# Row scatters kept out of values' products, empty rows scattered between the first expert blocks, silu in place

## The chip, the cores and the metric

The kernel runs on one core of a Trainium2 chip. Its time is the device time of one execution in microseconds; the time of a kernel is the median over its runs. PE is TensorE, DVE is VectorE, ACT is ScalarE, POOL is GpSimd and SP is SyncE. A name such as L705 is a line of the kernel before, which is also the line that its profile shows; the changed kernel's lines lie a few numbers off.

## The reference

The input x has 16 batches of 512 tokens of 256 numbers. The reference normalizes each token and adds to x an attention layer and a mixture of experts, both fed by the normalized tokens:

```python
xn = _layernorm(x, axis=-1)
x = x + _L0_attn_ref(xn, ...) + _L0_ffn_ref(xn, ...)

# attention: 16 heads of 16, rotary q and k, causal softmax
scores = einsum('bqhd,bkhd->bhqk', q, k) * scale          # masked above the diagonal
out = einsum('bhqk,bkhd->bqhd', softmax(scores), v).reshape(B, S, H * Dh)
return out @ Wo.T

# experts: 32 experts of hidden size 128, the best 4 of each token, and a shared expert of 512
topk_scores, topk_idx = top_k(softmax(flat @ router_w.T + router_bias), 4)
h = silu(einsum('nd,ehd->neh', flat, gate_w)) * einsum('nd,ehd->neh', flat, up_w)
out = (sel * topk_scores[:, :, None]).sum(axis=1)         # sel: the 4 chosen experts' outputs
out = out + silu(flat @ sgate_w.T) * (flat @ sup_w.T) @ sdown_w.T
```

Everything is float32.

## The kernel before

**One order for all.** The order of the work on every engine is written out by hand. The program is a sequence of some 350 rounds, and `for r in range(last)` emits them one after the other. A round begins with `cut()` and `scores(r)`: products of queries and keys for the attention (L840, twice: `sq` to find the row maxima on DVE, `sk` transposed to be exponentiated by ACT into a tile `pe`). `cut()` has GpSimd zero what lies above the diagonal in the `pe` of the round before (L866). Then come steps that were put into a round by `at(r, cost, step)`, and between them steps of the list `fill`, taken as they fit a level of PE work per round. Each engine has its own queue and works through it in order; SyncE's queue issues most of the DMAs, in order too.

**Attention.** A batch takes 20 rounds for `scores`, in two halves of heads `p`. Twelve rounds later `values(b, p, c)` multiplies the `pe` tiles by the values `va` (L886, 32 matmuls), for one quarter `c` of the heads at a time. These products fall into two of every ten rounds.

**Routing and scattering.** In rounds 0 to 35 tokens are normalized and routed, and each token's row of 265 numbers (the token, its four experts, their weights, its number) goes to `xn_d` in HBM. The experts' rows lie one expert after the other in `xs`, in half blocks of 128 rows. From round `R_SCATTER` = 36 to round 127 rows are scattered into `xs`: `reload(b)` has SyncE bring a batch's rows back into one of three `rows` tiles (L551), and puts 16 scatters of 128 rows each on the list `waiting`; `scatter(n)` has GpSimd issue the next n of these (L560, indirect DMAs). The counts per round are spread evenly:

```python
rows_in_all, rounds = B * NT * TOPK + E, R_MOE - 2 - R_SCATTER
at(R_MOE - 2 - rounds // 6, 0.0, scatter_empty)
n = (r + 1) * rows_in_all // rounds - gone
```

The `E` = 32 scatters at the end are `scatter_empty`: for each expert, an empty row is written to the unused rows of its last half block (`gaps`), so that these rows belong to a token number that doesn't count. PE works on attention and on the shared expert (`gate_up` L246, `down` L258, whose tokens come as `sxt` through SyncE, L233) in these rounds.

**Blocks.** At round `R_MOE` = 130 `begin_blocks` starts 144 blocks of 256 rows, two half blocks with an expert each. For block n, SyncE reads the rows `xb` from `xs` (`fetch_rows`, L640, five tiles) and the two experts' weights `w` (`fetch`, L647, four tiles); PE transposes (L654), multiplies by gate and up (L667), and by down (L691); GpSimd adds the results to `moe` in HBM with accumulating indirect DMAs (`add_up`, L705). The step `first(n)` issues, in this order, the rows of block n+4, the weights of block n+2, the sums of block n-3, and gate and up of block n. Blocks follow on each other until round 302, where the sums are combined and the last batches of attention are done.

**silu.** `glu` (L277 to L282) is used by the shared expert and by the blocks: ACT makes the tanh `th` (L279), DVE makes `gs` out of it (L281) and the product out of `gs` (L282).

Of the kernel before, what the change touches and what calls it, by code (L numbers as in the profile page):

```python
# [11 lines left out]
F32 = mybir.dt.float32  # L12
# [5 lines left out]
ALU = mybir.AluOpType  # L18
# [4 lines left out]
P = 128  # L23
B, S, D = 16, 512, 256
NT = S // P
T = B * NT
NH, DH, HP = 16, 16, 32
# [4 lines left out]
BLK, BC = 2 * HB, 2  # L32
# [40 lines left out]
def block_kernel(ctx: ExitStack, tc, x, wqkv, wo, rope, rw, rb, wexp, sg, su, sd, out):  # L73
# [202 lines left out]
    def glu(dst, ps, name):  # L276

        th = spool.tile([P, 2 * P], F32, tag="th", name=f"th_{name}", bufs=2)
        nc.scalar.activation(th, ps[:, 0, :], AF.Tanh, scale=0.5)  # L279
        gs = spool.tile([P, 2 * P], F32, tag="gs", name=f"gs_{name}", bufs=2)  # L280
        nc.vector.scalar_tensor_tensor(gs, th, 1.0, ps[:, 0, :], ALU.add, ALU.mult)  # L281
        nc.vector.scalar_tensor_tensor(dst, gs, 0.5, ps[:, 1, :], ALU.mult, ALU.mult)  # L282

    def interleaved_shared(halves, late=False, sums=None, xt=None):

# [190 lines left out]

    empty = epool.tile([P, ROW], F32, tag="empty", name="empty", bufs=1)
    nc.vector.memset(empty, 0.0)  # L480
    nc.gpsimd.tensor_copy(empty[:, ID_AT : ID_AT + 1].bitcast(I32), ids[:, T : T + 1])
    none = epool.tile([P, D], F32, tag="none", name="none", bufs=1)
# [74 lines left out]
    def scatter(most):  # L557
        for _ in range(min(most, len(waiting))):
            n, index, row = waiting.pop(0)
            nc.gpsimd.indirect_dma_start(  # L560
                out=views[n % NVIEWS],
                out_offset=bass.IndirectOffsetOnAxis(ap=index, axis=0),
                in_=row,
                in_offset=None,
            )

    def scatter_empty():
        waiting.extend((e, gaps[:, e : e + 1], empty) for e in range(E))


    def block_tables():
# [62 lines left out]
    def expert_steps(pool):  # L634

        w, xb, xt, ht, wrow, ybs, who = {}, {}, {}, {}, {}, {}, {}

        def fetch_rows(n):
            xb[n] = pool.tile([P, BC, ROW], F32, tag="xb", name=f"xb_{n}", bufs=5)
            nc.sync.dma_start(  # L640
                xb[n], xs[n * BLK : (n + 1) * BLK, :].rearrange("(c p) d -> p c d", p=P)
            )

        def fetch(n):
            w[n] = pool.tile([P, BC, 3 * D + 1], F32, tag="w", name=f"w_{n}", bufs=4)
            for c, e in enumerate(on_sync(where[n % P : n % P + 1, n // P, :], E - 1)):
                nc.sync.dma_start(w[n][:, c, :], wexp[bass.ds(e * P, P), :])  # L647

        def turned(n):
            pt = bank([P, 2, BLK], f"pxt_{n}")  # L650
            rows = xb[n]
            for c in range(BC):
                for dc in range(2):
                    nc.tensor.transpose(  # L654
                        pt[:, dc, c * P : (c + 1) * P], rows[:, c, dc * P : (dc + 1) * P], ident
                    )
            xt[n] = pool.tile([P, 2, BLK], F32, tag="xbt", name=f"xbt_{n}", bufs=2)
            nc.scalar.copy(xt[n], pt)  # L658

        def gate_up(n):  # L660
            pg = bank([P, 2, BLK], f"pg_{n}")
            rows = xt.pop(n)
            for u in range(2):
                for c in range(BC):
                    for dc in range(2):
                        at = (2 * u + dc) * H
                        nc.tensor.matmul(  # L667
                            pg[:, u, c * HB : (c + 1) * HB], lhsT=w[n][:, c, at : at + H],
                            rhs=rows[:, dc, c * HB : (c + 1) * HB],
                            start=(dc == 0), stop=(dc == 1),  # L670
                        )
            ht[n] = pool.tile([P, BLK], F32, tag="ht", name=f"ht_{n}", bufs=2)
            glu(ht[n], pg, f"e{n}")

            four = pool.tile([P, BC, TOPK], F32, tag="four", name=f"four_{n}", bufs=2)
            for c in range(BC):
                nc.vector.scalar_tensor_tensor(  # L677
                    four[:, c, :], xb[n][:, c, E_AT : E_AT + TOPK], w[n][:, c, 3 * D :],
                    xb[n][:, c, W_AT : W_AT + TOPK], ALU.is_equal, ALU.mult,
                )  # L680
            wrow[n] = pool.tile([P, BC], F32, tag="wrow", name=f"wrow_{n}", bufs=3)
            nc.vector.tensor_reduce(wrow[n], four, AX.X, ALU.add)

            who[n] = pool.tile([P, BC], I32, tag="who", name=f"who_{n}", bufs=6)
            nc.vector.tensor_copy(who[n], xb.pop(n)[:, :, ID_AT].bitcast(I32))

        def down(n):
            py = bank([P, BC, D], f"py_{n}")
            h = ht.pop(n)
            for c in range(BC):  # L690
                nc.tensor.matmul(  # L691
                    py[:, c, :], lhsT=h[:, c * P : (c + 1) * P], rhs=w[n][:, c, 2 * D : 3 * D],
                    start=True, stop=True,
                )
            w.pop(n)
            yb = pool.tile([P, BC, D], F32, tag="yb", name=f"yb_{n}", bufs=4)
            weight = wrow.pop(n)
            for c in range(BC):
                nc.scalar.mul(yb[:, c, :], py[:, c, :], weight[:, c : c + 1])  # L699
            ybs[n] = yb  # L700

        def add_up(n):
            yb, at = ybs.pop(n), who.pop(n)
            for c in range(BC):
                nc.gpsimd.indirect_dma_start(  # L705
                    out=moe[c],
                    out_offset=bass.IndirectOffsetOnAxis(ap=at[:, c : c + 1], axis=0),
                    in_=yb[:, c, :], in_offset=None, compute_op=ALU.add,
                )

        def first(n):
            if n == -2:
                for k in range(4):
                    fetch_rows(k)
                for k in range(2):
                    fetch(k)
            if 0 <= n + 4 < NBLK and n >= 0:
                fetch_rows(n + 4)
            if 0 <= n + 2 < NBLK and n >= 0:
                fetch(n + 2)  # L720
            if 0 <= n - 3 < NBLK:
                add_up(n - 3)
            if 0 <= n < NBLK:
                gate_up(n)

        out = []
        for n in range(-2, NBLK + 3):
            out.append((1.75 if 0 <= n < NBLK else 0.0, lambda n=n: first(n)))
            if 0 <= n + 2 < NBLK:
                out.append((0.45, lambda n=n: turned(n + 2)))  # L730
            if 0 <= n - 1 < NBLK:
                out.append((0.9, lambda n=n: down(n - 1)))
        return out
# [147 lines left out]
    def values(b, p, c):  # L881
        po = bank([P, S], f"po_{b}_{p}_{c}")
        for k in range(NT):
            j, col = PLACE_K[c, k]
            for g in range(4):
                nc.tensor.matmul(  # L886
                    po[g * HP : (g + 1) * HP, k * P :],
                    lhsT=va[b % 2][k][:, 8 * p + 4 * c + g, :],
                    rhs=pes[b, p, j, g // 2][:, g % 2, col : col + S - k * P],
                    start=(k == 0), stop=(k == NT - 1), skip_group_check=True,  # L890
                )
        oc = work.tile([P, S], F32, tag="oc", name=f"oc_{b}_{p}_{c}")
        nc.scalar.copy(oc, po)
        pos_o[b, p, c] = oc
# [51 lines left out]
            stores.append((half(out_v, b, i2), xr))  # L946


    events = {}

    def at(r, cost, step):
        events.setdefault(r, []).append((cost, step))
# [24 lines left out]
    for b in range(B):  # L977
        for p in range(2):
            r = 20 * b + 10 * p
            at(r + 10, 0.45, lambda b=b, p=p: maxima(b, p))  # L980
            for c, rv in ((0, r + LAG + 7), (1, r + LAG + 11)):
                at(rv, 2.3, lambda b=b, p=p, c=c: values(b, p, c))
                at(rv + 1, 0.45, lambda b=b, p=p, c=c: normalized(b, p, c))
            at(r + LAG + 13, 0.45, lambda b=b, p=p: turned(b, p))
        for i2 in range(2):
# [29 lines left out]
    empty_rows, experts = block_tables()  # L1015
    at(R_SCATTER + 5, 0.0, empty_rows)
    at(R_SCATTER + 7, 0.0, experts)
    rows_in_all, rounds = B * NT * TOPK + E, R_MOE - 2 - R_SCATTER
    for b in range(B):

        last = R_SCATTER + b * NT * TOPK * rounds // rows_in_all - 1
# [2 lines left out]
        at(first, 0.0, lambda b=b: place(b))  # L1024
        at(second, 0.0, lambda b=b: placed(b))
        at(R_SCATTER + max(0, b - 2) * NT * TOPK * rounds // rows_in_all, 0.0, lambda b=b: reload(b))
    at(R_MOE - 2 - rounds // 6, 0.0, scatter_empty)
    gone = 0
    for r in range(rounds):
        n = (r + 1) * rows_in_all // rounds - gone  # L1030
        at(R_SCATTER + r, 0.0, lambda n=n: scatter(n))
        gone += n

# [3 lines left out]
    at(R_LAST - 4, 0.0, load_late)  # L1037

    def begin_blocks():
        scatter(len(waiting))  # L1040
        stages.pop("rows").close()
        stages.pop("early").close()
        begin, *steps = expert_steps(open_pool("blocks"))
        fill[:] = [begin, *fill, *steps]
# [123 lines left out]
```

## Time and profile before

| | |
|---|---|
| median of 15 runs | 1782.51 us (1776.58 to 1790.38) |
| the profiled execution | 1783.11 us, of which the span is 1781.4 us |
| granted TensorE clock, mean | 0.992 |
| row scatters (L560) | 288: 256 of rows from 281.0 us, 32 of empty rows from 655.5 to 699.7 us |
| rows of blocks (L640) | 144 reads of 265 KB, from 704.0 to 1610.1 us |
| weights of blocks (L647) | 288 loads of 384.5 KB |

Times in the profile are microseconds from the span's start. A row of a group gives its busy time, the mean of one instruction, and the idle time of its engine just before it with what ended that. A wait is given as engine, line and what was waited for, then total, times and longest. A timeline row has the start and length of an instruction (or of several alike, x4) and, in brackets, the idle time before it and its releaser. In a table by stretches each stretch has its length, then the busy time of each engine, the granted clock, the share of the DMA engines and GB/s. The chain is the work that ended last, followed back from the end: at each step to what released it.

### The profile page before, as it was taken

To read this page: it belongs to the slowest core of one execution; us is meant where nothing else is said; L and a number is where in the kernel's file an instruction comes from. 1 tells how busy PE (TensorE), PEld (TensorE's weight loads), DVE (VectorE), ACT (ScalarE), POOL (GpSimd) and SP (SyncE) were. 2 spreads that over 40 slices of the span, in tenths; PEclk is the share of its full clock that TensorE was granted. 3 is DMA by queue.
4 is the path that set the end of the run, shared out by engine and by line. 5 is a ranking of instruction groups with operands and counts; after the bars stand their busy time and mean duration, and the time that the engine had idled before them with its cause. 6 is when DMAs were issued, how large, how long until landed. Compare 5 with 4: busy or idle time off the path is not lost.

```text
span 1781.4 us, 37880 instructions
## 1 busy us (share of the span) xinstructions
PE 1731.8 (97%) x13361; PEld 1237.2 (69%) x13361; DVE 1199.3 (67%) x4179; ACT 844.1 (47%) x1481; POOL 1050.9 (59%) x1419
## 2 busy tenths in 40 slices
PE   8899999999999999999999999999999999999898
PEld 6666766666666666777777777768778687777555
DVE  6778877776767665666666566575656656666585
ACT  3335533343434334455555555555555555555332
POOL 3345545888888886255656656565665656656221
PEclk9999999999999999999999999999999999999999
DMA  4354544456554535579798898988889888896498
GB/s 156 129 197 151 192 153 139 159 169 230 185 186 143 173 119 169 159 195 242 187 252 210 203 239 199 238 199 220 232 202 243 191 231 228 197 247 143 121 319 270
DMA packets 227518, 347.97 MB, mean 195 GB/s; under 512 B 22656, under 2 KB 165760, under 8 KB 227328
## 3 DMA queue, kind: packets, MB, share of 16 engines
q1 hardware_dynamic: 167424, 260.29, 46.2%
q0 software_dynamic: 55296, 76.86, 21.9%
q10 hardware_dynamic: 4608, 8.39, 1.2%
q8 instruction: 106, 1.74, 0.4%
q14 instruction: 84, 0.69, 0.1%
HBM read 218.12 MB, written 128.39 MB: 195 GB/s over the span
## 4 chain that ended last, share of the span: by engine, by line
PE 83%; DVE 6%; DMA 4%; POOL 3%; issue 1%; ACT 1%; SPq 0%; DVEq 0%; ACTq 0%; POOLq 0%
PE sq L840 16%; PE pg L667 15%; PE psgu L246 11%; PE py L691 7%; PE po L886 7%; PE pqk L766 6%; PE psd L258 5%; PE pxt L654 4%; PE pt L804 3%; PE pv L794 3%; PE pa L934 3%; POOL xs L560 2%; DVE junk L846 2%; PE pot L902 1%; DMA out<-sum 1%
## 5 line engine op out<-in xcount | busy, mean ns | idle before, releaser
L705 POOL DMA_INDIRECT moe<-yb,who x288 | 451.9, 1569 | 323.2 <-DMA moe<-yb,who 118.1
L846 DVE CUSTOM_DVE_ANT_0 junk<-sq,causal 128x256 bf16<-128x256 f32 (+3 forms) x1024 | 501.6, 490 | 205.8 <-PE sk L840 174.7
L854 ACT ACTIVATE pe<-sk 128x1024 f32<-128x1024 f32 x320 | 328.0, 1025 | 307.4 <-PE sk L840 303.8
L840 PE MATMUL sq<-kt,qt 16*128 16x384 f32 (+3 forms) x2048 | 365.2, 462 | 11.8 <-DVE top L846 11.6
L866 POOL TENSOR_SCALAR_AFFINE_SELECT pe<-pe 128x256 f32<-128x256 f32 x512 | 276.7, 695 | 160.9 <-ACT pe L854 155.9
L840 PE MATMUL sk<-qt,kt 18*128 18x512 f32 (+3 forms) x2048 | 365.2, 462 | 0.0
L560 POOL DMA_INDIRECT xs<-rows,pos x256 | 250.7, 979 | 80.3 <-issue 76.9
L667 PEld LDWEIGHTS pg<-xbt,w 128*128 128x128 f32 x2304 | 272.2, 191 | 34.0 <-issue 15.9
L667 PE MATMUL pg<-xbt,w 128*128 128x128 f32 x2304 | 288.3, 278 | 0.2 <-ACT xbt L658 0.2
L840 PEld LDWEIGHTS sq<-kt,qt 16*128 16x128 f32 x2048 | 174.5, 184 | 147.7 <-issue 54.0
L840 PEld LDWEIGHTS sk<-qt,kt 18*128 18x128 f32 x2048 | 174.3, 184 | 4.6 <-issue 2.9
L281 DVE SCALAR_TENSOR_TENSOR gs_e<-th_e,pg 128x256 f32<-128x256 f32 x144 | 60.6, 421 | 172.4 <-ACT th_e L279 171.8
L886 PE MATMUL po<-pe,va 128*32 128x512 f32 (+3 forms) x2048 | 151.9, 437 | 3.7 <-POOL pe L866 2.7
L691 PE MATMUL py<-w,ht 128*128 128x256 f32 x576 | 153.4, 389 | 1.4 <-DVE four L677 1.1
L246 PE MATMUL psgu<-sxt,sg_sb 128*128 128x256 f32 x496 | 140.2, 406 | 10.4 <-DMA sxt<-xt_d 7.3
L699 ACT ACTIVATE yb<-py,wrow 128x256 f32<-128x256 f32 x288 | 121.3, 474 | 36.9 <-PE py L691 35.5
L886 PEld LDWEIGHTS po<-pe,va 128*32 128x32 f32 x2048 | 59.8, 109 | 102.7 <-issue 78.5
L246 PE MATMUL psgu<-sxt,su_sb 128*128 128x256 f32 x496 | 130.7, 387 | 0.0
L258 PE MATMUL psd<-sd_sb,hs 128*128 128x256 f32 x512 | 126.9, 391 | 3.1 <-DVE hs L282 3.1
L279 ACT ACTIVATE th_e<-pg 128x256 f32<-128x256 f32 x144 | 55.3, 384 | 155.6 <-PE pg L667 155.6
L246 PEld LDWEIGHTS psgu<-sxt,sg_sb 128*128 128x128 f32 x496 | 87.1, 192 | 54.9 <-issue 33.2
L279 ACT ACTIVATE th_s<-psgu 128x256 f32<-128x256 f32 x128 | 49.2, 384 | 152.9 <-PE psgu L246 146.8
(152 smaller groups left out, 2449.6 us busy)
## 6 DMA issues: line engine op xcount, KB each, us to landing
w<-in_wexp SPq DMA_DIRECT2D x288, 384.5 KB, 4.8
xb<-xs SPq DMA_DIRECT2D x144, 265.0 KB, 3.7
sum<-moe SPq DMA_DIRECT2D x48, 256.0 KB, 5.0
xn_d<-xn SPq DMA_DIRECT2D x16, 530.0 KB
rows<-xn_d SPq DMA_DIRECT2D x16, 530.0 KB, 4.8
xt_d<-xt ACTq DMA_DIRECT2D x32, 256.0 KB, 2.0
sxt<-xt_d SPq DMA_DIRECT2D x31, 256.0 KB, 5.6
xn<-in_x SPq DMA_DIRECT2D x15, 512.0 KB, 4.2
```

The lines of the kernel that those rows point to most:

```text
L246: nc.tensor.matmul(ps[:, u, :], lhsT=w[:, c, m * P : (m + 1) * P], rhs=hold["xt"][:, c, :], start=(c == 0), stop=(c == 1),)
L258: nc.tensor.matmul(hold["py"][:, il, :], lhsT=hold["h"][:, m, il * P : (il + 1) * P], rhs=sd_sb[:, m, :], start=(m == 0), stop=(m == HS // ...
L560: nc.gpsimd.indirect_dma_start(out=views[n % NVIEWS], out_offset=bass.IndirectOffsetOnAxis(ap=index, axis=0), in_=row, in_offset=None,)
L667: nc.tensor.matmul(pg[:, u, c * HB : (c + 1) * HB], lhsT=w[n][:, c, at : at + H], rhs=rows[:, dc, c * HB : (c + 1) * HB], start=(dc == 0), ...
L691: nc.tensor.matmul(py[:, c, :], lhsT=h[:, c * P : (c + 1) * P], rhs=w[n][:, c, 2 * D : 3 * D], start=True, stop=True,)
L699: nc.scalar.mul(yb[:, c, :], py[:, c, :], weight[:, c : c + 1])
L705: nc.gpsimd.indirect_dma_start(out=moe[c], out_offset=bass.IndirectOffsetOnAxis(ap=at[:, c : c + 1], axis=0), in_=yb[:, c, :], in_offset=N ...
L840: nc.tensor.matmul(dst, lhsT=lhsT, rhs=rhs, start=True, stop=True)
L846: nc.vector.tensor_tensor_reduce(out=junk[:, :n], in0=sq[:, h, col : col + n], in1=causal[:, S - n :], scale=1.0, scalar=LOWEST, op0=ALU.a ...
L854: nc.scalar.activation(pe, st, AF.Exp, scale=DH ** -0.5)
L866: nc.gpsimd.affine_select(out=diag, in_=diag, compare_op=ALU.is_ge, fill=0.0, base=0, pattern=[[0, 2], [1, P]], channel_multiplier=-1,)
L886: nc.tensor.matmul(po[g * HP : (g + 1) * HP, k * P :], lhsT=va[b % 2][k][:, 8 * p + 4 * c + g, :], rhs=pes[b, p, j, g // 2][:, g % 2, col ...
```

## The change

In `glu` the intermediate stays in `th`, and `gs` is gone. The tile `empty` moves to the pool that lasts for the whole kernel, since empty rows are now scattered while blocks run. The 32 scatters of empty rows leave the rounds up to 127: the first eight experts' go in `begin_blocks`, and those of two more experts in each of `first(0)` to `first(11)`, just ahead of the block read whose half blocks they may lie in. The 256 scatters of rows are shared out with a weight of 0.6 for rounds with values' products and 1 for the others. After values' products, while scatters are waiting, GpSimd writes a zero to one number of `va` that is zero already.

```diff
@@ glu
         th = spool.tile([P, 2 * P], F32, tag="th", name=f"th_{name}", bufs=2)
         nc.scalar.activation(th, ps[:, 0, :], AF.Tanh, scale=0.5)
-        gs = spool.tile([P, 2 * P], F32, tag="gs", name=f"gs_{name}", bufs=2)
-        nc.vector.scalar_tensor_tensor(gs, th, 1.0, ps[:, 0, :], ALU.add, ALU.mult)
-        nc.vector.scalar_tensor_tensor(dst, gs, 0.5, ps[:, 1, :], ALU.mult, ALU.mult)
+        nc.vector.scalar_tensor_tensor(th, th, 1.0, ps[:, 0, :], ALU.add, ALU.mult)
+        nc.vector.scalar_tensor_tensor(dst, th, 0.5, ps[:, 1, :], ALU.mult, ALU.mult)
...
-    empty = epool.tile([P, ROW], F32, tag="empty", name="empty", bufs=1)
+    empty = const.tile([P, ROW], F32, tag="empty", name="empty")
...
-    def scatter_empty():
-        waiting.extend((e, gaps[:, e : e + 1], empty) for e in range(E))
+    def scatter_empty(first, end):
+
+        scatter(len(waiting))
+        waiting.extend((e, gaps[:, e : e + 1], empty) for e in range(first, min(end, E)))
+        scatter(len(waiting))
...
@@ first(n)
             if 0 <= n + 4 < NBLK and n >= 0:
+                scatter_empty(BC * (n + 4), BC * (n + 5))
                 fetch_rows(n + 4)
             if 0 <= n + 2 < NBLK and n >= 0:
                 fetch(n + 2)
...
@@ values(b, p, c), after the matmuls
+        if waiting:
+            nc.gpsimd.memset(va[b % 2][NT - 1][:1, NH - 1, HP - 1 : HP], 0.0)
         oc = work.tile([P, S], F32, tag="oc", name=f"oc_{b}_{p}_{c}")
...
-    rows_in_all, rounds = B * NT * TOPK + E, R_MOE - 2 - R_SCATTER
+    rows_in_all, rounds = B * NT * TOPK, R_MOE - 2 - R_SCATTER
...
-    at(R_MOE - 2 - rounds // 6, 0.0, scatter_empty)
-    gone = 0
+    shares = [0.6 if "values" in kinds.get(R_SCATTER + r, ()) else 1.0 for r in range(rounds)]
+    gone, share = 0, 0.0
     for r in range(rounds):
-        n = (r + 1) * rows_in_all // rounds - gone
+        share += shares[r]
+        n = round(rows_in_all * share / sum(shares)) - gone
         at(R_SCATTER + r, 0.0, lambda n=n: scatter(n))
         gone += n
...
     def begin_blocks():
-        scatter(len(waiting))
+        scatter_empty(0, 4 * BC)
```

`kinds` holds the rounds into which `values` was put. `reload(b)` takes its round from `rows_in_all`, and so moves by up to eight rounds back.

More of the change, by code (lines that the diff above doesn't have):

```diff
@@ L946, in finish @@
             stores.append((half(out_v, b, i2), xr))
-    events = {}
+    events, kinds = {}, {}
     def at(r, cost, step):
@@ L982, in block_kernel @@
                 at(rv, 2.3, lambda b=b, p=p, c=c: values(b, p, c))
+                kinds.setdefault(rv, set()).add("values")
                 at(rv + 1, 0.45, lambda b=b, p=p, c=c: normalized(b, p, c))
```

## The prediction

> **What bounds the kernel now.** I read the busy table first, then the values' products by stretches, then waits, chain and timelines of the scatters' stage (281 to 700 us) and of the first blocks (700 to 840 us).
>
> ```profile
> PE 1731.8 (97%) x13361; PEld 1237.2 (69%) x13361; DVE 1199.3 (67%) x4179; ACT 844.1 (47%) x1481; POOL 1050.9 (59%) x1419
> ```
>
> PE is the bound as a whole, so what the change can save is what PE idles where the change acts, and what it can lose is new PE idling. The answer for 281:700 alone, sum line:
>
> ```profile
> 281.00:700.00 419.00, 410.96 (x2980) 275.93 (x2980) 298.03 (x919) 163.20 (x243) 341.71 (x434) 1.00 0.50 167
> ```
>
> PE idles 419.00 - 410.96 = 8.0 us there. Who waited, in the same stretch:
>
> ```profile
> POOL xs L560 <- issue: 85.3, 278, 13.0
> PE sq L840 <- DVE top L846: 5.6, 11, 1.6
> PE psgu L246 <- DMA sxt<-xt_d: 2.6, 1, 2.6
> POOL pe L866 <- ACT pe L854: 0.5, 1, 0.5
> ```
>
> GpSimd waits for data 0.5 us; the rest of its idling is the 0.30 us between two scatters (and 13 us before the first). It is full in this stage, yet costs PE little: of the 8.0 us, 5.6 are DVE's and 2.6 one late sxt load. The chain of waits shows where that one comes from (start us, us, what):
>
> ```profile
> 419.27 2.50 DMA xs<-rows,pos
> ...
> 422.36 5.22 DMA sxt<-xt_d
> ```
>
> A scatter started at 419.27 and landed 2.50 us later; SyncE's reload of rows waited for that, and the sxt load stood behind it in SyncE's queue.
>
> Values' products (L886) by stretches: PE busy, then weight loads.
>
> ```profile
> 180.00:240.00 60.00, 4.72 (x64) 1.88 (x64) 1.00 0.51 175
> 300.00:360.00 60.00, 7.08 (x96) 2.81 (x96) 1.00 0.55 177
> 960.00:1020.00 60.00, 4.72 (x64) 1.88 (x64) 1.00 0.85 207
> ```
>
> One group of 32 takes 4.72/2 = 2.36 us before the scatters, 7.08/3 = 2.36 during them and 2.36 after: scatters don't slow it. Keeping scatters out of these products is worth nothing to PE by this trace.
>
> The first blocks, timelines of GpSimd, SyncE and PE (start us, us, engine, line):
>
> ```profile
> 699.69 0.96 POOL L560 DMA_INDIRECT xs<-empty,gaps  x1 [0.30 <-issue]
> 702.58 0.41 POOL L866 TENSOR_SCALAR_AFFINE_SELECT pe<-pe 128x256 f32<-128x256 f32 x1 [1.15 <-ACT pe L854]
> 718.10 0.77 POOL L866 TENSOR_SCALAR_AFFINE_SELECT pe<-pe 128x256 f32<-128x256 f32 x2 [4.74 <-ACT pe L854]
> ```
> ```profile
> 703.99 1.90 SPq L640 DMA_DIRECT2D xb<-xs  x4
> ...
> 714.92 0.46 SPq L640 DMA_DIRECT2D xb<-xs  x1
> 716.39 0.90 SPq L647 DMA_DIRECT2D w<-in_wexp  x2
> ```
> ```profile
> 724.66 2.05 PE L667 MATMUL pg<-xbt,w 128*128 128x128 f32 x16 [0.24 <-ACT xbt L658]
> ...
> 739.21 2.05 PE L667 MATMUL pg<-xbt,w 128*128 128x128 f32 x16
> ...
> 809.51 2.05 PE L667 MATMUL pg<-xbt,w 128*128 128x128 f32 x16
> ```
>
> The last empty scatter starts at 699.69, and SyncE reads the first four blocks at 703.99, when it has landed (4.3 us from its start). PE begins gate_up of block 0 at 724.66, of block 2 at 739.21, of block 13 at 809.51 (the 14th group of 16 at L667): (809.51 - 724.66)/13 = 6.5 us a block, with next to nothing waited for.
>
> **The change part by part.**
>
> *silu in place.* The same 272 pairs of vector instructions of 0.42 us. A tanh two calls later now waits for the second of the pair, not the first: 0.42 us later on a tile of two buffers, while two successive calls lie some 4 us apart (699.44 and 703.30 in the timeline), and ScalarE waits for PE's pg (155.6 us) and psgu (146.8 us) anyway. Nothing; were every wait exposed, 272 x 0.42 = 114 us, but PE's in-order products stand in between.
>
> *The empty row's tile moved to another pool.* No instruction changes; nothing.
>
> *Shares of scatters.* The stage of 92 rounds issues 256 instead of 288 scatters, 1 or 2 instead of 3 or 4 in the 18 rounds with values' products. GpSimd gets 32 x (0.96 + 0.30) = 40 us free of 419. What PE can gain is the 2.6 us behind the reload, since its 5.6 us on DVE top have no scatter in them. Ends: 0 (the reloads move against the sxt loads and another one is late) and 8.0 (all of the stage's idling). I take -2.6.
>
> *The memset after values' products.* Only head 15's columns of the last chunk are written, and only the group with p = 1 and c = 1 reads them. In the built instruction lists 4 of the 18 memsets wait for PE, 14 do not. So it mostly does not hold scatters back at all. Where it does, what is queued behind it on GpSimd is one or two scatters and the next round's cut of pe; the scatters' reload on SyncE and values' products two rounds later wait for these. It costs GpSimd at most one round, 419/92 = 4.6 us, four times, against the 40 us freed; the memset itself is bounded by the 0.125 us of the constant memset of 128x16 (L179). PE: 0, at worst one more late sxt load (2.6).
>
> *The empty rows between the blocks.* Eight scatters go in one burst ahead of the first block read, then two ahead of each of the reads of blocks 4 to 15. All of xs is one tensor to the dependencies: in the built lists each of these 12 pairs on GpSimd waits for the previous block read (xb) to land, and each xb read on SyncE waits for the pair just issued. Before, the xb reads waited only for DVE's who, five buffers back. That is a closed loop: pair, landing, xb read, landing, next pair. Queued behind SyncE's wait is the weight fetch of block n+2 (L647), and gate_up of block n+2 waits for that; behind GpSimd's wait are the cuts of pe and the accumulating scatters into moe (L705), who have three blocks' slack.
>
> The start: GpSimd reaches the burst after the cut at 702.58, so the first scatter starts at 703.2, the eighth at 703.2 + 7 x 1.26 = 712.0. Landing from a scatter's start: 2.2 to 2.6 us in the quiet stage (the chain's 2.50), 4.3 us for the one at 699.69 with a 512 KB and a 256 KB load just issued. In the loop two weight loads of 384 KB are in flight, so I take 3.4, between. The four xb reads are issued at 715.4 to 717.3 and land by 721 (median 4.4 us in 700:850, 3.7 over all 144). The first pair then runs at 721.3 and 722.6 and lands at 726: block 4 is read at 726 instead of 714.92.
>
> The loop: 1.26 between the two scatters + 3.4 landing + 3.7 xb landing + 0.2 for the two wake-ups = 8.6 us, against 6.5 us a block on PE. Ends: 1.26 + 2.2 + 2.7 + 0.2 = 6.4 (the shortest landing of xs's own loads is 2.7) and 1.26 + 4.3 + 6.2 + 0.2 = 12.0 (the longest is 6.2).
>
> After 11 turns block 15's xb is read at 726 + 11 x 8.6 = 820.6. The weights of block 13 are issued 1.2 and 1.65 us later and land after 4.8: 827.0. PE wanted them at 809.51: late by 17.5 us. For block 2 the same sum gives 726 + 6.4 = 732.4, before 739.21: the lead of 6.8 us is eaten at 2.1 us a block, from about block 6 on PE waits. PE is in order and has no later idling to give it back in the block stage, so 17.5 us stay.
>
> The Trainium skill, page "DMA: Bandwidth & Descriptors", section "Anatomy of one DMA — SWDGE (gpsimd) path", says that a DMA issued by GpSimd takes about 2.0 us plus its bytes at 436 GB/s, most of it completion, whatever the size; that speaks against chaining small ones. For 128 rows of 1060 bytes that is an estimate of 2.3 us, close to the trace's quiet 2.2 to 2.6 and under its 4.3. By it the loop would be 7.5 us and block 13 late by about 5 us, which would make +3 us in all.
>
> The sum: +17.5 - 2.6 = +14.9 on the profiled execution's 1783.1 us (span 1781.4, 1.7 around it): 1798.0. The median of the 15 runs is 0.6 lower, so 1797 for the median.
>
> **Rivals.**
>
> 1. *The loop keeps pace and the change wins.* Place: the 12 pairs. It decides where 726 + 11p + 6.4 stays under 809.5, that is a loop p of 7.0 us or less. For it: quiet landings (2.2 + 2.7 give 6.4). Against: weights and accumulating scatters are in flight in each turn. Then only the scatters' stage counts: 1779.9 with 2.6 us gained, 1774.5 with all 8.0.
> 2. *A longer loop.* At 1.26 + 4.3 + 4.4 + 0.2 = 10.2 us a turn block 15 is read at 838.2, block 13 late by 35 us: 1815. For it: accumulating scatters of 1.57 us each stand between the pairs from the fourth on, and GpSimd already waits 114 us for their landings in 700:1620. Against: the stalled PE leaves the DMA engines freer.
> 3. *The change does not do what it says, and nothing moves.* True of 14 memsets, but the loop stands whatever they do. Alone it would be 1780 to 1783.
>
> **How the numbers follow.** About 0.2%, 3.6 us, is what a measurement of this kernel can tell. Forecast (loop 7.6 to 9.8 us) 0.64; longer loop 0.15; together 0.79 slower, with 0.01 from rival 3 with a late load. Loop of 7.0 or less with over 3.6 us gained 0.12, faster. The rest, 0.08, lies within 3.6 us: a loop of about 7.2 us pays back just the 2.6. The range goes from 1778 (loop hidden, 4.5 us gained) to 1818 (the longer loop).
>
> **What would show it.** In the changed profile: xb<-xs issues 8 to 9 us apart between 726 and 821, then bunched; SyncE waiting for DMA xs<-empty,gaps and GpSimd's L559 waiting for DMA xb<-xs, about 12 times; PE idle at gate_up behind DMA w<-in_wexp between 770 and 840, some 17 us in all; no sxt wait in the scatters' stage; values' groups still 2.36 us. I am wrong if the issues stay 6 to 7 us apart, if PE stays 99% busy in that stretch, or if PE's idling sits in the scatters' stage instead.

## The result, and the profile after

The changed kernel takes 1802.12 us (median of 8 runs, 1795.1 to 1805.27), the kernel before 1782.99 us (40 runs): a ratio of 1.0106, 95% interval 1.0091 to 1.012, so 18.9 us slower [16.2, 21.4]. 1797 was predicted, in a range of 1778 to 1818. The profiled execution took 1800.0 us with a span of 1798.2, 16.8 us over that of before. The chip of these runs is not on record; on the chip of the first four experiments the kernel before takes 1786.99 us, close to this. On two other chips, where the rest of the experiments ran, the kernel before itself takes 1846 to 1851 us, and there the sign turns, which is told below. Every measured time is compared with runs of the kernel before beside it; ratios are the recorded ones, which are not the quotients of the two medians, and the differences in us with their intervals are worked out from them.

The lines of the changed kernel lie up to five off: L559 is the scatters, L642 the rows of blocks, L649 the weights, L669 gate and up, L889 values' products, L707 the adds, L869 the cut, L898 the memset.

The busy table of the page:

```profile
PE 1735.5 (97%) x13361; PEld 1241.5 (69%) x13361; DVE 1210.4 (67%) x4179; ACT 843.0 (47%) x1481; POOL 1044.7 (58%) x1437
```

PE has the same instructions and 3.7 us more busy time; the other 13 us of the longer span are idle. By stretches (length, then busy PE, PEld, DVE, ACT, POOL, granted clock, DMA share, GB/s), the scatters' stage and the first blocks of the changed kernel:

```profile
281.00:700.00 419.00, 412.53 (x2990) 277.82 (x2989) 297.14 (x916) 163.47 (x245) 308.47 (x423) 1.00 0.47 157
770.00:860.00 90.00, 74.43 (x573) 55.78 (x575) 40.56 (x153) 37.87 (x69) 57.05 (x57) 0.92 0.82 215
```

and the second stretch of the kernel before:

```profile
770.00:860.00 90.00, 89.77 (x755) 67.18 (x754) 55.84 (x214) 51.11 (x92) 52.02 (x52) 1.00 0.89 226
```

In the scatters' stage PE idles 6.5 us instead of 8.0. In the 90 us of the blocks it idles 15.6 us instead of 0.2, and does the rest at a mean clock of 0.92. From 860 to 1640 us the two traces agree (777.58 and 777.15 us busy). So the time goes in one place. Who waited in 700:870 (engine, line, awaited: total us, times, longest), on GpSimd, PE and SyncE:

```profile
POOL xs L559 <- DMA xb<-xs: 30.5, 11, 6.4
PE pg L669 <- DMA w<-in_wexp: 15.3, 6, 4.0
```
```profile
SPq L642 <- DMA xs<-empty,gaps: 89.0, 15, 12.5
```

That is the loop, closed: GpSimd waits for the block read, SyncE for the pair of scatters, PE for the weights queued behind SyncE's wait. SyncE's issues and GpSimd's pairs (start us, us):

```profile
722.74 0.38 SPq L642 DMA_DIRECT2D xb<-xs  x1
723.83 0.90 SPq L649 DMA_DIRECT2D w<-in_wexp  x2
...
819.75 0.38 SPq L642 DMA_DIRECT2D xb<-xs  x1
820.93 0.87 SPq L649 DMA_DIRECT2D w<-in_wexp  x2
821.90 0.38 SPq L642 DMA_DIRECT2D xb<-xs  x1
```
```profile
726.09 0.97 POOL L559 DMA_INDIRECT xs<-empty,gaps  x1 [6.37 <-DMA xb<-xs]
727.37 0.96 POOL L559 DMA_INDIRECT xs<-empty,gaps  x1 [0.30 <-issue]
```

Twelve reads from 722.74 to 819.75: (819.75 - 722.74)/11 = 8.82 us a turn. Single turns take 7.45 to 10.16 us: the first three 7.61 on average, and the eight after GpSimd's adds have begun (744.13) 9.27. The next read, with no pair ahead of it, follows 2.15 us later: the bunching that the prediction named. PE's timeline at gate_up:

```profile
720.00 2.05 PE L669 MATMUL pg<-xbt,w 128*128 128x128 f32 x16 [0.24 <-ACT xbt L660]
...
771.92 2.05 PE L669 MATMUL pg<-xbt,w 128*128 128x128 f32 x16
780.55 3.78 PE L669 MATMUL pg<-xbt,w 128*128 128x128 f32 x16 [3.34 <-DMA w<-in_wexp]
```

Up to block 7 (771.92, the eighth) each start lies where it did relative to the first; from block 8 on PE waits. Block 0 to block 13 takes 825.72 - 720.00 = 105.7 us, against 84.85 before. The chain of waits shows the loss turn by turn (start us, us, what):

```profile
793.57 4.32 DMA w<-in_wexp
797.88 0.14 issue
798.02 3.72 PE pg L669 x16
...
820.93 4.65 DMA w<-in_wexp
825.58 0.14 issue
825.72 3.67 PE pg L669 x16
```

The 16 matmuls after a wait take 3.4 to 3.8 us instead of 2.05. The granted clock tells why, in short stretches of the changed kernel:

```profile
798.00:801.80 3.80, 3.78 (x19) 3.75 (x20) 0.00 (x0) 0.02 (x1) 2.98 (x3) 0.55 0.28 79
825.70:829.40 3.70, 3.69 (x18) 3.50 (x19) 0.00 (x0) 0.00 (x0) 1.92 (x3) 0.57 1.06 349
830.50:834.00 3.50, 3.50 (x29) 2.49 (x27) 1.77 (x9) 1.59 (x4) 1.67 (x2) 1.00 1.09 344
```

3.72 x 0.55 = 2.05: the same work at little more than half the clock, for the first 3.5 us after a wait, and at full clock after that. Four such groups (from 780.55, 798.02, 815.74 and 825.72; 3.78, 3.72, 3.40 and 3.67 us) make 6.4 us. With the 15.3 us of waits that is 21.7 of the 22.5 us by which the way from gate_up of block 0 to that of block 14 is longer than before (110.5 and 88.05 us).

Values' products and the memsets, the products in two stretches (PE, weight loads) and the waits of 281:700:

```profile
180.00:240.00 60.00, 4.72 (x64) 1.88 (x64) 1.00 0.52 178
300.00:360.00 60.00, 7.08 (x96) 2.82 (x96) 1.00 0.52 170
```
```profile
POOL va L898 <- PE po L889: 19.4, 4, 5.5
PE sq L843 <- DVE top L849: 6.0, 11, 1.0
```

Still 2.36 us a group. Four of the 18 memsets wait; no wait for sxt is left.

### The profile page after: what moved, and what is told of

Same layout as the page of the kernel before. It is cut to its first block, busy times and chain, and to the rows that moved or that the text cites. A ratio compares the mean times of both kernels' runs of the same rounds, so it can differ in the third digit from the quotient of the medians.

```text
span 1798.2 us, 37782 instructions
## 1 busy us (share of the span) xinstructions
PE 1735.5 (97%) x13361; PEld 1241.5 (69%) x13361; DVE 1210.4 (67%) x4179; ACT 843.0 (47%) x1481; POOL 1044.7 (58%) x1437
## 4 chain that ended last, share of the span: by engine, by line
PE 84%; DVE 8%; DMA 5%; issue 1%; ACT 1%; SPq 1%; POOL 1%; DVEq 0%; ACTq 0%
PE sq L843 16%; PE pg L669 15%; PE psgu L246 11%; PE py L693 7%; PE po L889 7%; PE pqk L769 6%; PE psd L258 6%; PE pxt L656 4%; PE pt L807 3%; PE pa L941 3%; PE pv L797 3%; DVE junk L849 2%; DMA w<-in_wexp 2%; DMA out<-sum 1%; PE pot L909 1%
## 5 line engine op out<-in xcount | busy, mean ns | idle before, releaser
L707 POOL DMA_INDIRECT moe<-yb,who x288 | 450.8, 1565 | 317.6 <-DMA moe<-yb,who 105.8
L843 PE MATMUL sq<-kt,qt 16*128 16x384 f32 (+3 forms) x2048 | 365.3, 462 | 15.5 <-DVE top L849 15.3
L869 POOL TENSOR_SCALAR_AFFINE_SELECT pe<-pe 128x256 f32<-128x256 f32 x512 | 272.0, 692 | 135.2 <-ACT pe L857 134.0
L669 PEld LDWEIGHTS pg<-xbt,w 128*128 128x128 f32 x2304 | 278.0, 195 | 50.4 <-issue 33.5
L669 PE MATMUL pg<-xbt,w 128*128 128x128 f32 x2304 | 295.0, 282 | 15.6 <-DMA w<-in_wexp 15.3
L559 POOL DMA_INDIRECT xs<-rows,pos x256 | 250.2, 977 | 87.6 <-issue 77.5
L280 DVE SCALAR_TENSOR_TENSOR th_e<-th_e,pg 128x256 f32<-128x256 f32 x144 | 60.6, 421 | 185.0 <-ACT th_e L279 184.8
L889 PE MATMUL po<-pe,va 128*32 128x512 f32 (+3 forms) x2048 | 153.0, 439 | 4.4 <-POOL pe L869 3.4
L889 PEld LDWEIGHTS po<-pe,va 128*32 128x32 f32 x2048 | 60.1, 110 | 104.3 <-issue 79.7
L693 PEld LDWEIGHTS py<-w,ht 128*128 128x128 f32 x576 | 99.8, 190 | 30.0 <-issue 9.9
```

The source lines that it names most:

```text
L559: nc.gpsimd.indirect_dma_start(out=views[n % NVIEWS], out_offset=bass.IndirectOffsetOnAxis(ap=index, axis=0), in_=row, in_offset=None,)
L669: nc.tensor.matmul(pg[:, u, c * HB : (c + 1) * HB], lhsT=w[n][:, c, at : at + H], rhs=rows[:, dc, c * HB : (c + 1) * HB], start=(dc == 0), ...
L693: nc.tensor.matmul(py[:, c, :], lhsT=h[:, c * P : (c + 1) * P], rhs=w[n][:, c, 2 * D : 3 * D], start=True, stop=True,)
L707: nc.gpsimd.indirect_dma_start(out=moe[c], out_offset=bass.IndirectOffsetOnAxis(ap=at[:, c : c + 1], axis=0), in_=yb[:, c, :], in_offset=N ...
L843: nc.tensor.matmul(dst, lhsT=lhsT, rhs=rhs, start=True, stop=True)
L869: nc.gpsimd.affine_select(out=diag, in_=diag, compare_op=ALU.is_ge, fill=0.0, base=0, pattern=[[0, 2], [1, P]], channel_multiplier=-1,)
```

## The experiments

The theory: the loop of pairs and reads makes the loss, by late weights. Rivals: the scatters' own time on GpSimd makes it; holding scatters back makes or hides some of it. Four kernels ran first, where the kernel before took 1786.99 us (17 runs). A trace shows one execution: those of one_a_block (1804.1 us), four_every_second (1811.37) and hold_all (1834.13) are among the slowest of their kernels, those of pairs_elsewhere (1790.56) and empty_rows_early (1831.31) the fastest.

**loop_alone.** The kernel before, with silu in place and `empty` in the lasting pool; the scatters' stage is left alone, and twelve pairs write empty rows a second time ahead of the reads. `scatter_again` issues the indirect DMAs for two experts.

```diff
             if 0 <= n + 4 < NBLK and n >= 0:
+                scatter_again(BC * (n + 4), BC * (n + 5))
                 fetch_rows(n + 4)
```

> The kernel before (silu in place, the empty tile kept) with its 32 empty scatters where they were, and 12 further pairs issued ahead of the reads of blocks 4 to 15 that write the same empty rows into xs a second time. Theory (the closed loop pair, landing, block read, landing): 11 turns of 8.8 us from a first read at about 723, weights of block 13 some 16 us late, in all 14 to 22 us slower than before. Rival (the burst of eight, or fewer scatters in the earlier rounds, made the loss): within 3 us of before.

Measured 1803.57 us, ratio 1.0107 [1.0083, 1.0131]: +19.1 us. The turn is 8.95 us (8.64 for the first three, 9.07 after) and block 0 to block 13 takes 103.6 us. The waits of 700:870:

```profile
POOL xs L572 <- DMA xb<-xs: 24.1, 10, 3.5
PE pg L675 <- DMA w<-in_wexp: 11.0, 5, 4.7
```

The pairs alone make the whole loss; the rest of the change adds nothing to it and takes nothing off that can be told.

**pairs_elsewhere.** The same 24 extra scatters in the same places, into tensors that nobody reads, at rows that follow on each other.

```diff
+    spares = [dram.tile([E * P, ROW], F32, ...) for k in range(8)]
...
-                out=views[e % NVIEWS],
+                out=spares[e % 8],
```

> As loop_alone, with the same 24 scatters at the same places, but into tensors that nobody reads, so that block reads do not wait for them nor they for block reads. Theory (the loop): 0 to 3 us slower than before. Rival (GpSimd's time and the DMA engines' load of 24 scatters between the blocks are the cost): as much as loop_alone, 14 to 22 us.

Measured 1796.58 us, 1.0057 [1.0035, 1.0079]: +10.2 us [6.3, 14.1], which no theory had. Reads are early again and block 0 to block 14 goes at before's pace (722.16 to 810.21), and the next block takes 13.5 us instead of 8.0. GpSimd's and PE's lines in that place:

```profile
808.50 1.58 POOL L716 DMA_INDIRECT moe<-yb,who  x1 [0.30 <-issue]
809.52 1.36 POOL L878 TENSOR_SCALAR_AFFINE_SELECT pe<-pe 128x256 f32<-128x256 f32 x2
814.71 1.58 POOL L716 DMA_INDIRECT moe<-yb,who  x1 [3.83 <-DMA moe<-yb,who]
```
```profile
PE po L898 <- POOL pe L878: 4.7, 2, 3.8
```

A turn on GpSimd holds two scatters (2.5 us), two adds (2 x 1.86 = 3.7) and cuts of about 0.9: 7.1 us against 6.5 us a block. By this sum its queue falls behind, and the rows show the last step: an add waits 3.83 us for an earlier add to land, the cut behind it is late, and values' products wait for the cut. So without the loop the scatters would not have been free: by this time half of the loss would have come another way. With the loop PE waits for the weights first, and the two don't add up.

**one_a_block.** As loop_alone, with one scatter a turn: `scatter_again(n + 8, n + 9 if n < 12 else 0)`.

> As loop_alone, with one scatter instead of two ahead of each of the 12 block reads. Theory: a turn loses one 1.28 us spacing, 8.8 to about 7.5 us against 6.5 us a block; 11 turns end 14 us earlier, so block 13 is late by 1 to 4 us and the whole 1 to 5 us slower than before. Rival (cost per scatter): half of loop_alone, 7 to 11 us slower.

Measured 1793.12 us, 1.0028 [1.0009, 1.0046]: +5.0 us. The turn is 7.87 us, block 0 to block 13 takes 90.1 us (+5.3), and PE's wait for weights has shrunk:

```profile
PE pg L675 <- DMA w<-in_wexp: 3.7, 4, 2.5
```

One issue and its gap less (1.3 us) shortens the turn by 1.1 us and takes off three quarters of the loss: what exceeds PE's pace is what costs.

**four_every_second.** The changed kernel with four experts ahead of every second read, so that there are six turns and not twelve.

```diff
-                scatter_empty(BC * (n + 4), BC * (n + 5))
+                if n % 2 == 0:
+                    scatter_empty(BC * (n + 4), BC * (n + 6))
```

> The changed kernel with four experts' empty rows ahead of every second block read instead of two ahead of each. Theory: a turn is 3.8 us of spacing, 2.6 to 3.4 landing, 2.1 to the second read, 3.7 landing and 0.2, 12.4 to 13.2 us for two blocks, 6.2 to 6.6 a block against 6.5: late by 0 to 4 us, so 3 us faster to 4 us slower than before, 15 to 22 us faster than the changed kernel. Rival (number of scatters between the blocks counts): as slow as the changed kernel, 19 us over before.

Measured 1800.88 us, 1.007 [1.0047, 1.0094]: +12.5 us, a miss. Turns take 16.4 us per two blocks, from 728.01 to 809.95. The pairs wait for reads only twice (9.8 us); GpSimd waits for its own adds instead:

```profile
POOL moe L707 <- DMA moe<-yb,who: 11.2, 6, 3.0
POOL xs L559 <- DMA xb<-xs: 9.8, 2, 5.6
PE pg L669 <- DMA w<-in_wexp: 10.7, 4, 4.0
```

With fewer landings GpSimd's queue mostly sets the turn, as these waits have it: four scatters (5.1 us), two pairs of adds (7.4), cuts and the adds' own landings. It is like what pairs_elsewhere showed, here ahead of the reads.

The second four ran on another chip (before: 1850.95 us, 29 runs). The kernel before left no trace there; silu_alone's stands in for it.

**gpsimd_time.** silu in place, and five memsets of 128x512 on GpSimd in each of the twelve places: time, but no DMA.

```diff
             if 0 <= n + 4 < NBLK and n >= 0:
+                if n < 12:
+                    for _ in range(5): nc.gpsimd.memset(idle, 0.0)
                 fetch_rows(n + 4)
```

> The kernel before (silu in place) with five memsets of 128x512 on GpSimd (5 x 0.52 = 2.6 us, the time of a pair of scatters with its gaps) where pairs_elsewhere has its 12 pairs; no DMA. Theory of a second limit (GpSimd has more than a block's time to do per block once a pair is added, so its cuts of pe come late and values' products wait): as pairs_elsewhere, 5 to 11 us slower than before, with PE waiting for pe at values' products around 815 us. Rival (the pairs' bytes load the DMA engines, and accumulating scatters land late for that): 0 to 3 us.

Measured 1856.74 us, 1.0008 [0.9981, 1.0036]: +1.5 us [-3.5, +6.7], while the medians lie 5.8 us apart. The time does not decide: the interval holds the rival and the lower end of what the theory expected. The trace says more. Block 18 still comes 112.7 us after block 0 (112.1 in silu_alone), but block 19 comes 18.5 us after block 18 instead of 11.1. GpSimd's and PE's lines there:

```profile
900.32 1.56 POOL L710 DMA_INDIRECT moe<-yb,who  x1 [3.62 <-DMA moe<-yb,who]
```
```profile
904.26 1.69 PE L893 MATMUL po<-pe,va 128*32 128x384 f32 x24 [4.03 <-POOL pe L873]
```

It is the stall of pairs_elsewhere, four blocks later: an add waits for an earlier add to land, and values' products for the cut behind it; the granted clock is 0.50 to 0.66 in the 8 us after that. So this trace shows that time on GpSimd can end in such a stall with no DMA added; the times alone do not show it.

**no_memset.** The changed kernel without the memset.

```diff
-        if waiting:
-            nc.gpsimd.memset(va[b % 2][NT - 1][:1, NH - 1, HP - 1 : HP], 0.0)
```

> The changed kernel without the memset after values' products. Theory (nothing hangs on it): within 3 us of the changed kernel, 17 to 21 us slower than before; GpSimd's four waits for values' products (19 us in the changed profile) are gone. Rival (the memset relieves values' products): more than 3 us slower than the changed kernel.

Measured 1833.54 us, 0.9895 [0.9865, 0.9925]: 19.4 us faster than before, where 17 to 21 us slower was expected: a miss. The loop costs what it did (block 0 to block 13 takes 101.7 us, +16.9), so something larger was gained ahead of it: the first gate_up starts at 758.34, in silu_alone at 785.94. The changed kernel itself did not run on this chip, so that the rival is not settled here.

**empty_rows_early.** The changed kernel with the 32 empty rows back in the scatters' stage: silu, shares and memset are left.

```diff
-                scatter_empty(BC * (n + 4), BC * (n + 5))
...
-        scatter_empty(0, 4 * BC)
+        scatter(len(waiting))
```

> The changed kernel with the 32 empty scatters back in the rounds up to 127, so with silu in place, the shares and the memset alone. Theory: the loop is gone and with it the loss; GpSimd is as full as before in these rounds and has the four waits of 19 us on top, so its last scatters come up to 19 us later against some 14 us of slack: 0 to 8 us slower than before. Rival (the loss is in the earlier rounds): 15 us slower or more.

Measured 1841.45 us, 0.9952 [0.9929, 0.9974]: 8.9 us faster, where 0 to 8 us slower was expected: a miss. Block 0 to block 13 takes 84.85 us, before's number: no pairs, no loss. The first gate_up starts at 776.09, 9.9 us ahead of silu_alone's.

**silu_alone.** The three lines of `glu`, nothing else.

> The kernel before with silu's intermediate in place and nothing else. Every theory: within 3 us of before.

Measured 1845.69 us, 0.9985 [0.996, 1.0011]: no difference that can be told. Its trace stands closest to the kernel before on that chip and shows what differs there. The scatters' stage, and two engines' waits in it:

```profile
281.00:700.00 419.00, 381.01 (x2582) 251.32 (x2575) 260.42 (x798) 138.47 (x209) 294.58 (x376) 0.95 0.46 149
```
```profile
ACT oc L892 <- remote: 39.5, 6, 7.2
DVE junk L845 <- remote: 24.6, 6, 7.6
```

PE idles 38 us where it idled 8 on the first chip, and gets through 13% fewer instructions, at a mean granted clock of 0.95 instead of 1.00. Up to 281 us PE is as busy as there (257.8 and 258.3 us), and the first gate_up starts 61.3 us later (785.94 and 724.66), which is the whole difference of the two executions (spans of 1841.0 and 1781.4 us). So what sets this chip apart lies between 281 us and the first block. "remote" means that the profile finds no releaser. One such place, in the timeline:

```profile
560.42 2.36 PE L885 MATMUL po<-pe,va 128*32 128x512 f32 x32
...
562.70 0.96 POOL L559 DMA_INDIRECT xs<-rows,pos  x1 [0.30 <-issue]
...
568.84 0.58 ACT L892 COPY oc<-po 128x512 f32<-128x512 f32 x1 [7.23 <-remote]
568.98 0.56 DVE L845 CUSTOM_DVE_ANT_0 junk<-sq,causal 128x384 bf16<-128x384 f32 x1 [4.52 <-remote]
```

Values' products end at 562.8, and the copy that needs nothing but them starts at 568.8; DVE, which needs the scores after them, starts in nearly the same moment, after GpSimd has issued scatter after scatter up to 567.8. The granted clock is 1.00 from 560.4 to 568.8, so a slower clock is not what makes this copy late, and PE's own records go on: the next scores start at 562.96. In the traces of before, after and loop_alone that copy starts 0.06 to 0.08 us after the last product in all 22 cases of 281:790. Here, in 281:800, it does so in 4 of 20 cases, and is over 3 us late in 11.

The last four ran on a third chip (before: 1846.08 us, 24 runs), to see what the parts are worth where this happens.

**changed_again.** The changed kernel.

> The changed kernel itself, timed beside the parts of it in the same comparison. Theory A (the loop in the first blocks decides, the scatter stage gives at most 1 us): 17 to 22 us slower than before, gate_up of block 0 to block 13 some 102 to 106 us instead of 84.85. Theory B (where values' products are followed late, as in silu_alone and empty_rows_early, in which ScalarE's copy began up to 7 us after the last product, thinner scatters bring back part of that): the blocks still lose 17 to 20 us, but the first block's gate_up starts 20 to 28 us earlier than in before, and the whole is between 10 us faster and 2 us slower. Which of them holds depends on whether before's scatter stage has such late copies where this is run.

**without_memset_again.** The edit of no_memset.

> The changed kernel without the one-element memset. Theory A (the memset only makes 4 of 18 groups of scatters wait, 19.4 us of GpSimd's time that nothing else wanted): within 2 us of changed_again. Theory B (the wait keeps late copies away): 4 to 15 us slower than changed_again, and more waits of ScalarE's copy of values over 5 us than in it. Rival C (the wait costs time: scatters held back pile up behind it): 3 to 8 us faster than changed_again.

**hold_all.** empty_rows_early, with the memset on a head that the group itself has read, so that each of the 18 waits for PE:

```diff
-            nc.gpsimd.memset(va[b % 2][NT - 1][:1, NH - 1, HP - 1 : HP], 0.0)
+            nc.gpsimd.memset(va[b % 2][NT - 1][:1, 8 * p + 4 * c + 3, HP - 1 : HP], 0.0)
```

> The empty rows stay in the scatters' stage, as before the change (no loop in the blocks: gate_up of block 0 to block 13 84.9 us); the shares are those of the change; the memset goes to the head that the group itself reads last, so that GpSimd waits for TensorE at all 18 groups of values and not at 4. Theory A (holding is worth nothing): 0 to 6 us slower than before, since 18 waits of 3 to 5 us take 50 to 90 us of a queue that has some 400 us of work in 419 us, and scatters end later. Theory B (held scatters bring values' products back to their pace): no wait of ScalarE's copy of values over 5 us is left, and the time is 5 to 20 us under before's.

**shares_only.** empty_rows_early without the memset.

> silu in place and the shares of 0.6 alone: no memset, and the empty rows stay in the scatters' stage, so no loop in the blocks (gate_up of block 0 to block 13 84.9 us). Theory A: within 3 us of before. Theory B: 3 to 12 us faster than before. If it is faster than before and than changed_again, it is the version to keep.

| | us | ratio to before | first gate_up | block 0 to 13 | late copies: over 1 us, longest |
|---|---|---|---|---|---|
| changed_again | 1836.44 | 0.9927 [0.9897, 0.9956] | 758.9 | 102.0 | 11 of 21, 6.6 us |
| without_memset_again | 1835.09 | 0.9922 [0.989, 0.9954] | 755.3 | 102.5 | 15 of 21, 4.5 us |
| hold_all | 1825.48 | 0.9874 [0.9832, 0.9916] | 770.3 | 84.9 | 0 of 20, 0.7 us |
| shares_only | 1842.2 | 0.9972 [0.9943, 1.0001] | 777.0 | 84.9 | 14 of 20, 6.4 us |

The change makes the kernel faster here, by 13.5 us [8.1, 19.0], more than Theory B's 10, and the loop's loss is still in it (+17.1 us to block 13). Against shares_only it starts the blocks 18.0 us earlier, and the loop takes all of that back: block 22 starts at 921.92 and 921.80. The two traced executions took 1837.95 and 1836.95 us, and the 5.8 us between the medians lie in no stage of these traces. shares_only itself is 5.2 us faster than before [-0.2, 10.5], which can't be told from nothing. The memset as it stands is worth nothing that can be told (1.4 us between the first two, Theory A). The memset that really waits keeps scatters out of values' products, as the title of the change has it. The waits of hold_all in 281:720:

```profile
POOL va L897 <- PE po L888: 36.3, 16, 6.2
ACT pe L856 <- remote: 20.3, 7, 4.8
ACT oc L899 <- PE po L888: 16.3, 10, 3.4
```

ScalarE's waits for values are put down to values again, none to "remote", and the time is 23.3 us under before's [15.5, 31.0] and, by the medians, 16.7 under shares_only's, from which it differs in the memset alone. So on this chip scatters issued beside values' products do hold up the copies that follow, and holding the scatters cures that; the theory that holding is worth nothing falls here. It cures no more than the copies: ScalarE's exponentials still wait 20.3 us for "remote", PE still idles 29.1 us in 281:700 (33.9 in shares_only), and the first gate_up comes 6.7 us earlier, so that most of the 16.7 us is not accounted for by the two traces (1834.13 and 1836.95 us). hold_all beats both kernels where it ran; on the chip of the prediction it was not run, and there the copies had no lateness to cure.

What stays open: whether on those chips the products themselves end late or only their signal does (ends of matmuls are modelled); what makes the waits for "remote" that are left in hold_all, whose first gate_up still comes 45 us after the first chip's; and why the kernel with fewer scatters starts its blocks 18 us ahead of shares_only there, while on the first chip they start 4.7 us ahead of before's.

## Why the prediction was right

*The loop, right.* The turn was 8.82 us for 8.6. Its terms: the second scatter started 1.29 us after the first (1.26), landings took 3.68 us from its start (2.67 to 4.91; 3.4 taken), and from a read's issue to the next pair 3.91 passed (3.9). The first read of block 4 was at 722.74, not 726: the burst began at 698.50 and not at 703.2, and of that 3.6 us lay ahead of the whole stage, whose first scatter started at 277.4 instead of 281.0 us. That the mean turn met the sum is in part luck. The sum has one turn for all, and the trace has 7.6 us for the first three and 9.3 for the rest, with both landings longer once the adds had begun (from the second scatter to the read 2.92 us and then 3.87, from the read to the next pair 3.41 and then 4.10). So PE waited from block 8 on and not from about block 6.

*The late weights, right.* Block 13 was to start when its weights land, at 827.0, and started at 825.72, 16.2 us after before's 809.51. Against its own first block that is 20.9 us late where the sum had 17.5: the first block came 4.66 us earlier and the weights 1.3, and 17.5 + 4.66 - 1.3 = 20.9. What the sum left out is the clock. The three slow groups before block 13 only shortened the waits behind them, since the loop sets when weights come; the last one's 1.6 us stayed, and 20.9 + 1.6 = 22.5. The Trainium skill, page "TensorE: Matmul & The Clock Gate", section "What's actually happening" in its Part 1, says that TensorE's clock falls to half after an idle window of about 3.4 us and comes back after as long a busy one. The trace agrees in the 3.5 us, and shows the fall after waits of 3.34 and 3.99 us, but after one of 2.78 us too (the group at 815.74, clock 0.58), and in loop_alone after one of 2.37 us (16 matmuls in 3.71 us, clock 0.53).

*The landing time, better by the row than by the page.* The Trainium skill's page "DMA: Bandwidth & Descriptors", section "Anatomy of one DMA — SWDGE (gpsimd) path", gave the prediction its estimate of 2.3 us, by which the loss would have been 3 us. Landings under the load of the blocks measured 3.68.

*That GpSimd's cuts and adds "have three blocks' slack": the step that failed.* It priced GpSimd's own time at nothing beside the loop. pairs_elsewhere measured 10.2 us for the same scatters with no loop at all, and gpsimd_time's trace has a like stall without their DMAs. By the sum above the slack is eaten by 0.6 us a block. It did not spoil the forecast, since the loop's wait comes first, but the first rival left it out: by this measure a loop that keeps pace would have given some 1790, not 1780.

*The scatters' stage: -2.6 predicted, too little to tell.* The sxt wait is gone, as said, and PE idles 1.5 us less in 281:700. The first gate_up came 4.66 us earlier, of which 3.6 lay ahead of 281 us. But in loop_alone, pairs_elsewhere and one_a_block, whose scatters' stage is that of before, it came at 723.01, 722.16 and 726.45 us (before: 724.66), so that a gain of 1 or 2 us is lost among them. The memset: four waits of 18, costing PE nothing, as said. silu: nothing that can be told.

*"Keeping scatters out of these products is worth nothing to PE by this trace": true of this trace, not of the kernel.* It rested on the duration of a group, 2.36 us, which stays 2.36 where the copies are late (the group at 560.42). What would have told is the time from the last product to its copy, and the trace of before has no late one. The forecast's sign holds for the chip that was traced; on the third chip the same kernel was 13.5 us faster, which nothing in the prediction foresaw.

## What to carry to other kernels

Before moving small writes in front of a read of the same tensor, ask whether the next write must wait for that read: if so, a cheap burst becomes a closed loop, and its turn (issue, landing, read, landing) has to be set against the time of a block, not its issue time against an engine's idle share. Give a moved instruction's own time on its queue a budget per block, too. And ask of a reading of one engine's group times what it can't show: here the time until the next engine took the result.

## What the runs showed that was not expected

After waits of 2.78 to 3.99 us in the changed kernel TensorE ran its next 16 matmuls at a granted clock of 0.54 to 0.58, in 3.4 to 3.8 us instead of 2.05; in loop_alone it did so after 2.37 us too. And the same kernel took 1783 to 1787 us in the first runs and 1846 to 1851 on two other chips. There ScalarE's copy after values' products started up to 6.8 us (in gpsimd_time) after the last product while GpSimd issued indirect scatters, against 0.06 to 0.08 us on the first, and at most 0.7 us once the scatters waited for the products.
